# Hidden units of a mixture-of-experts layer dealt to partitions, weight loads in halves, and products of ones at the start

## The chip, the cores and the metric

The kernel runs on one core of a Trainium2 chip. Five engines work side by side there: TensorE (PE, with its weight loads shown apart as PEld), VectorE (DVE), ScalarE (ACT), GpSimd (POOL) and SyncE (SP), which issues most of the DMAs. The metric is the device time of one execution in microseconds (us). Smaller is better.

## The reference

One block of a diffusion-style transformer, all in fp32, on x of 8 sequences of 512 tokens with 256 channels:

```python
mod = (silu(c) @ wmod).reshape(8, 6, 1, 256)      # sa, ca, ga, sb, cb, gb
ga = (2 * (ga >= 0) - 1) * maximum(abs(ga), 0.25)  # gb in the same way
h = layernorm(x) * (1 + ca) + sa
x = x + ga * linear_attention(h)                   # 16 heads of 16, rope, elu + 1, causal
h = layernorm(x) * (1 + cb) + sb
x = x + gb * experts(h)                            # 8 experts, the best 2 of each token
```

An expert is `gelu(h @ w1[e]) @ w2[e]` with w1 of 256 x 1024 and w2 of 1024 x 256. The router's softmax gives each token two experts and their weights, which are normalised to a sum of 1.

## The kernel before

**Attention.** A sequence is worked on in four chunks of 128 tokens. Each chunk goes through `early` (normalise, transpose, project to q, k, v, rope, elu), `middle` (cumulative sums for the denominator, transposes), `late` (scores, state, outputs, the output projection) and `rows_of` (the second normalisation, one row per token for the experts, router logits). After the fourth chunk `route` finds the two experts of each token and scatters its rows by indirect DMA (POOL) into lists by expert in HBM, called `slots`.

**Experts.** A block is one unit of 128 rows (a single) or two (a pair) of one expert's list. `fetch` (L1289) issues on SP the block's weights (`weights1` L1302, `weights2` L1307: 1 MB each) and its rows (L1324). `turn_rows` transposes the rows on DVE. Then, in `experts` (L1448), groups of products make h_ps (inner units on partitions, tokens along the free dimension), ACT applies gelu into g, and `second` (L1369) multiplies g with w2 into y_ps. `finish` scales y and POOL adds it by indirect DMA to the tokens in HBM. The weights have three buffers each. Of the 40 blocks that run, 27 are pairs and 13 are singles; the second half of the execution is experts alone, the first half attention with some experts in between.

**How the inner units lie.** w1 is loaded as [128 channels, 2, 1024]; the stationary operand of a product is 128 neighbouring columns, `w1_sb[:, k, ts(each * j + i, P)]`. So inner unit n*128 + p lies on partition p of the n-th group, and w2 is loaded to match: partition p takes eight rows of 1 KB each, 128 rows apart.

**Startup.** `modulation` (L622) multiplies silu(c) by wmod in two parts. The second part (modr_ps) gives the gates and the second shift and scale: a copy by ACT, then five POOL instructions (add 1 to one quarter; sign, twice; maximum; product), and a store to HBM (modd), from which each sequence loads its rows.

**What sets the order.** Nothing is issued in source order. The class `Plan` (L159) collects all work with a cost in us, a level (smaller goes first) and what it depends on; its `run` (L233) goes through time once, gives each engine the ready work of the smallest level for which buffers are free, and the instructions are issued in that order, engine by engine. A changed cost, level or buffer anywhere can thus move instructions on every engine. PSUM has three groups of banks: `early` (3), `late` (4), `y` (1).

Of the kernel before, what the change touches and what calls it, by code (L numbers as in the profile page):

```python
# [18 lines left out]
P = 128  # L19
HEADS = 16  # L20
# [6 lines left out]
FLOOR = 0.25  # L27
LARGE = 2.0**96
XS = 4

LEVEL = {
    "open": 0, "early": 0, "middle": 0, "late": 0, "rows": 0, "route": 0, "scatter": 0, "plan": 0
# [126 lines left out]
class Plan:  # L159
    SIGNAL = 0.25  # L160
    NEXT = {"DVE": 0.08, "ACT": 0.1}
    DRAIN = {"PE": 0.16}
    TABLE = 1.3
    RATE = 0.26

    def __init__(self, tc, before=None):
        self.tc, self.works, self.level, self.open = tc, [], 0, None
# [65 lines left out]
    def run(self):  # L233
        for w in self.works:
            w.behind -= self.before
            w.waits = len(w.behind)
            for b in w.behind:
                b.ahead.append(w)
            for t in w.tiles:
                t.left = len(t.users)  # L240
        slots = {}
        for w in self.works:
            for t in w.tiles:
                slots.setdefault((id(t.pool), t.tag), t.bufs)
        free = {e: 0.0 for e in {w.engine for w in self.works}}
        ready = {e: [] for e in free}
        events, table, channel, order, clock = [], None, 0.0, [], 0.0

        port = {"DVE": 0.0, "POOL": 0.0}
        for w in self.works:  # L250
            if not w.waits:
                heappush(ready[w.engine], w)
        todo = len(self.works)
        while todo or events:
            for e in sorted(ready):
                if free[e] > clock or not ready[e]:
                    continue
                passed, chosen = [], None
                while ready[e]:
                    w = heappop(ready[e])  # L260
                    if w.port and e == "DVE" and port["POOL"] > clock:
                        passed.append(w)
                        continue
                    need = {}
                    for t in w.tiles:
                        if not t.held:
                            k = (id(t.pool), t.tag)
                            need[k] = need.get(k, 0) + 1
                    if all(slots[k] >= n for k, n in need.items()):
                        chosen = w  # L270
                        break
                    passed.append(w)
                for p_ in passed:
                    heappush(ready[e], p_)
                if chosen is None:
                    continue
                w = chosen
                for t in w.tiles:
                    if not t.held:
                        t.held = True  # L280
                        slots[(id(t.pool), t.tag)] -= 1
                us = w.us
                if w.table is not None and w.table != table:
                    us += self.TABLE
                    table = w.table
                if w.port:
                    if e == "POOL":
                        us += max(port["DVE"] - clock, 0.0)
                    port[e] = clock + us
                free[e] = clock + max(us - self.NEXT.get(e, 0.0), 0.0)  # L290
                w.start, w.stop = clock, clock + us + self.DRAIN.get(e, 0.0)
                if w.bytes:
                    channel = max(channel, w.stop + w.landing) + w.bytes / self.RATE
                    done = channel
                else:
                    done = w.stop + w.landing
                heappush(events, (done, 0, w.at, w))
                heappush(events, (done + self.SIGNAL, 1, w.at, w))
                heappush(events, (free[e], 2, w.at, None))
                order.append(w)  # L300
                todo -= 1
            if not events:
                if todo:
                    left = sorted(w.at for w in self.works if not hasattr(w, "start"))
                    raise RuntimeError(f"no way on: {todo} left, first {left[:5]}")
                break
            clock = events[0][0]
            while events and events[0][0] <= clock:
                _, kind, _, w = heappop(events)
                if kind == 0:  # L310
                    for t in w.tiles:
                        t.left -= 1
                        if not t.left:
                            slots[(id(t.pool), t.tag)] += 1
                    for a in w.ahead:
                        if a.engine == w.engine and not w.bytes:
                            a.waits -= 1
                            if not a.waits:
                                heappush(ready[a.engine], a)
                elif kind == 1:  # L320
                    for a in w.ahead:
                        if a.engine != w.engine or w.bytes:
                            a.waits -= 1
                            if not a.waits:
                                heappush(ready[a.engine], a)
        self.order = order
        return order
# [25 lines left out]
def kernel(  # L353
# [78 lines left out]
    def bank(name, tag, bufs):  # L432
        return L.tile(ps, [P, 512], tag, name, bufs)
# [4 lines left out]
    def early_bank(name):  # L438
        return bank(name, "early", 3)
# [22 lines left out]
    def pool(method, out_, *args, us=None, **kw):  # L462
        if us is None:
            us = 0.12 + 0.0024 * out_.free
        return L.call("POOL", us, method, out_, *args, port=method in two, **kw)

    def copy(out_, in_):
        return L.call("ACT", 0.22 + 0.00075 * out_.free, A.copy, out_, in_)

    def product(out_, a, b, **kw):  # L470
        L.call("PE", 0.0, T.matmul, out_, a, b, **kw)
# [130 lines left out]
    nc.vector.memset(zeros, 0.0)  # L602


    silu = L.tile(cpool, [P, KD, Q], "silu", "silu")
    nc.vector.memset(silu.now(), 0.0)

# [14 lines left out]
    def modulation():  # L622
# [18 lines left out]
        with L.group("PE", 1.1):  # L641
            for k in range(KD):
                for j in range(P // Q):
# [2 lines left out]
                        wm[k][:, (2 + rows_by[j]) * D : (3 + rows_by[j]) * D].of(1),  # L646
                        start=(k == 0), stop=(k == KD - 1), skip_group_check=True,
                    )
        copy(modr, r_ps[:, :D])
        one_more = modr[quarters[rows_by.index(CB)]].of("cb")  # L650
        pool(G.tensor_scalar_add, one_more, one_more, 1.0)

        sgn, mag = (L.tile(p2, [P, D], "sm", t, 4) for t in ("sgn", "mag"))
        sgn, mag, g = sgn[: 2 * Q], mag[: 2 * Q], modr[: 2 * Q].of("g")
        act(mag, g, AF.Abs)
        pool(G.tensor_scalar, sgn, g, 0.0, 2.0, op0=ALU.is_ge, op1=ALU.mult)
        pool(G.tensor_scalar_add, sgn, sgn, -1.0)
        pool(G.tensor_scalar_max, mag, mag, FLOOR)
        pool(G.tensor_mul, g, sgn, mag)
        modded = L.tile(dram, [1, 1], "modded", "modded")  # L660

        def store():
# [12 lines left out]

        stored = L.do("SP", 2.0, store, r=[modr], w=[modded], landing=2.5)
        return modded, stored


    def moments(xs_, n, name):  # L680
# [105 lines left out]
    def middle(q, c):  # L786
# [9 lines left out]
                product(cum_ps[:, :D], ones, q.ksum, start=False, stop=True)  # L796
        q3 = q_.rearrange("p (h d) -> p h d", d=HD)
        dve(V.tensor_mul, qk, cum_ps[:, :D].rearrange("p (h d) -> p h d", d=HD), q3)
        den = L.tile(p2, [P, HEADS, 1], "den", f"den_{n}", 2)
        dve(V.tensor_reduce, den, qk, us=0.42, axis=AX.X, op=ALU.add)  # L800

        dve(V.reciprocal, den, den, us=0.24)
# [26 lines left out]
    def late(q, c):  # L829
# [21 lines left out]

        nxt = None
        if c < NC - 1:
            st_ps = early_bank(f"st_ps_{n}")
            kv = L.tile(p2, [P, KD, PAIR], "kv", f"kv_{n}", 2)
            with L.group("PE", 0.26, hold=[kv]):
                for g in range(KD):
# [43 lines left out]
                        )  # L901
        q.state = nxt
        copy(oT, oT_ps[:, :D])
        a_ps = early_bank(f"a_ps_{n}")
        with L.group("PE", 0.86):
            for k in range(KD):
                product(
# [377 lines left out]

    X = Expert()
    TOP = -50

    def fetch(block):  # L1289
        n, nt = block.n, block.nt  # L1290
# [6 lines left out]
        r = L.tile(pb, [P, 2, ROW - D], "r", f"r_{n}", 3)  # L1297
        reg = {}

        def weights1():  # L1300
            reg["e"] = nc.sync.value_load(block.expert_i.now(), min_val=0, max_val=E - 1)
            nc.sync.dma_start(  # L1302
                out=w1_sb.now(), in_=w1[ds(reg["e"], 1)].rearrange("o (k p) h -> p (o k) h", p=P)
            )

        def weights2():
            nc.sync.dma_start(  # L1307
                out=w2_sb.now(), in_=w2[ds(reg["e"], 1)].rearrange("o (n p) d -> p (o n) d", p=P)
            )

        def rows():
# [14 lines left out]
                apart(got, [s for s in scattered if s not in needed], "those are of later blocks")  # L1326
                gathered.append(got)

        L.do("SP", 0.6, weights1, r=[block.expert_i], w=[w1_sb], landing=2.0, mb=1.0)
        L.do("SP", 0.4, weights2, r=[block.expert_i], w=[w2_sb], landing=2.0, mb=1.0)  # L1330
        L.do("SP", 1.0, rows, r=[block.slot], w=[sx, r], after=block.seen, landing=2.0, mb=0.35 * nt)
        return block, w1_sb, w2_sb, sx, r

    def turn_rows(fetched):
# [113 lines left out]
    def experts(blocks):  # L1448
# [4 lines left out]
        while X.fetched or X.turned:  # L1453
# [11 lines left out]
            for j in range(groups):  # L1465
# [3 lines left out]
                with L.group("PE", 0.2165 * each * KD * nt, hold=[g]):  # L1469
                    for i in range(each):  # L1470
                        for k in range(KD):
                            product(
                                h_ps[:, i * w : (i + 1) * w], w1_sb[:, k, ts(each * j + i, P)],
                                xT[:, k, :w], start=(k == 0), stop=(k == KD - 1),
                            )
                L.level = TOP
# [131 lines left out]
```

## Time and profile before

| | us |
|---|---|
| median of 13 runs | 790.79 (790.02 to 793.68) |
| the profiled execution | 791.07 |
| its span, first to last instruction | 789.4 |
| PE busy / DVE busy / POOL busy / ACT busy | 753.7 / 383.8 / 317.0 / 283.3 |
| mean granted TensorE clock | 0.986 |

The span is what the engines' instructions cover; 1.7 us of the profiled execution lie around it. A fp32 product appears in the trace as two weight loads (PEld) and two matmuls (PE). A weight load can run while the matmul before it still streams. DMA issues stand on SP's queue (SPq) and are not counted as busy.

### The profile page before, as it was taken

To read this page: it belongs to the slowest core of one execution; us is meant where nothing else is said; L and a number is where in the kernel's file an instruction comes from. 1 tells how busy PE (TensorE), PEld (TensorE's weight loads), DVE (VectorE), ACT (ScalarE), POOL (GpSimd) and SP (SyncE) were. 2 spreads that over 40 slices of the span, in tenths; PEclk is the share of its full clock that TensorE was granted. 3 is DMA by queue.
4 is the path that set the end of the run, shared out by engine and by line. 5 is a ranking of instruction groups with operands and counts; after the bars stand their busy time and mean duration, and the time that the engine had idled before them with its cause. 6 is when DMAs were issued, how large, how long until landed. Compare 5 with 4: busy or idle time off the path is not lost.

```text
span 789.4 us, 16224 instructions
## 1 busy us (share of the span) xinstructions
PE 753.7 (95%) x5824; PEld 618.7 (78%) x5824; DVE 383.8 (49%) x1315; ACT 283.3 (36%) x584; POOL 317.0 (40%) x482
## 2 busy tenths in 40 slices
PE   5699979999799999999999999999999999999995
PEld 2477657768587787878888888888989889888884
DVE  3888969898597978878463101111111111111110
ACT  4456445657566665564231111111111111111110
POOL 5835643746445383736238421213212122130332
PEclk9899998999999999999999999999999999999998
DMA  7422370886637556546889987876876978879951
GB/s 243 108 57 75 107 223 19 309 233 200 158 110 206 177 191 194 181 132 202 253 222 279 293 233 205 227 209 195 249 210 210 274 220 256 222 207 316 287 104 22
DMA packets 132195, 154.31 MB, mean 195 GB/s; under 512 B 43640, under 2 KB 115344, under 8 KB 131984
## 3 DMA queue, kind: packets, MB, share of 16 engines
q1 hardware_dynamic: 116704, 125.24, 52.9%
q0 software_dynamic: 15408, 28.00, 14.0%
q8 instruction: 48, 0.79, 0.4%
q14 instruction: 35, 0.29, 0.1%
HBM read 120.19 MB, written 37.20 MB: 199 GB/s over the span
## 4 chain that ended last, share of the span: by engine, by line
PE 79%; POOL 6%; DMA 6%; DVE 4%; issue 3%; SPq 1%; ACT 1%; POOLq 0%; DVEq 0%
PE h_ps L225 26%; PE y_ps L225 25%; PE qk_ps L225 5%; PE oT_ps L225 5%; PE s_ps L225 4%; PE v_ps L225 4%; DMA out_dram<-y,to 3%; PE a_ps L225 3%; PE cum_ps L225 3%; PE qkT_ps L225 2%; DVE sm L225 2%; DMA out_dram<-acc 2%; POOL out_dram L1412 1%; POOL slots L1044 1%; POOL f L225 1%
## 5 line engine op out<-in xcount | busy, mean ns | idle before, releaser
L225 PE MATMUL h_ps<-xT,w 128*128 128x256 f32 (+1 forms) x1280 | 255.1, 346 | 0.0
L225 PE MATMUL y_ps<-w,g 128*128 128x256 f32 x1072 | 253.9, 380 | 0.0
L225 PEld LDWEIGHTS h_ps<-xT,w 128*128 128x128 f32 x1280 | 213.1, 191 | 24.5 <-issue 1.4
L225 PEld LDWEIGHTS y_ps<-w,g 128*128 128x128 f32 x1072 | 201.8, 190 | 27.1 <-issue 0.4
L225 ACT ACTIVATE g<-h_ps 128x512 f32<-128x512 f32 x134 | 80.0, 597 | 327.2 <-PE h_ps L225 327.1
L1412 POOL DMA_INDIRECT acc<-y,to x56 | 89.3, 1595 | 230.9 <-DVE y L225 193.2
L225 DVE SCALAR_TENSOR_TENSOR y<-y_ps,cw,r 128x256 f32<-128x256 f32 x67 | 30.0, 480 | 161.5 <-PE y_ps L225 161.4
L225 DVE STREAM_TRANSPOSE xT<-sx 128x512 f32<-128x512 f32 (+1 forms) x40 | 25.0, 624 | 150.9 <-PE h_ps L225 82.6
L225 DVE TENSOR_TENSOR sm<-s_ps,causal 128x512 f32<-128x512 f32 x128 | 83.1, 681 | 9.7 <-PE s_ps L225 9.6
L1044 POOL DMA_INDIRECT slots<-row,slot x64 | 64.1, 1002 | 27.3 <-issue 13.1
L225 PE MATMUL qk_ps<-wqkv_sb,hT 128*128 128x512 f32 x128 | 62.4, 611 | 0.7 <-DVE qk L225 0.5
L225 POOL TENSOR_TENSOR f<-f,t 128x512 f32<-128x512 f32 x32 | 43.0, 1344 | 37.8 <-DVE t L225 30.3
L225 PEld LDWEIGHTS s_ps<-qT,kT 32*128 32x128 f32 x1024 | 33.3, 194 | 10.4 <-issue 9.9
L225 ACT ACT_TABLE_LOAD x31 | 39.8, 1283 | 4.5 <-DMA cs<-in_cT_dram 3.1
L1412 POOL DMA_INDIRECT out_dram<-y,to x11 | 17.1, 1555 | 56.6 <-DMA out_dram<-acc 22.9
L225 PE MATMUL s_ps<-qT,kT 32*128 32x128 f32 x1024 | 39.6, 292 | 0.0
L225 PE MATMUL oT_ps<-sm,vz 128*32 128x128 f32 x1024 | 37.4, 277 | 1.6 <-DVE sm L225 1.4
L225 PEld LDWEIGHTS qk_ps<-wqkv_sb,hT 128*128 128x128 f32 x128 | 23.4, 194 | 19.3 <-issue 16.0
L225 PE MATMUL v_ps<-wqkv_sb,hT 128*128 128x256 f32 x128 | 36.1, 405 | 1.9 <-ACT hT L225 1.1
L225 PEld LDWEIGHTS oT_ps<-sm,vz 128*32 128x32 f32 x1024 | 27.2, 109 | 11.3 <-issue 7.2
L225 PE MATMUL a_ps<-wo,oT 128*128 128x256 f32 x128 | 33.7, 386 | 0.0
L225 ACT ACTIVATE t<-f 128x512 f32<-128x512 f32 x32 | 20.3, 634 | 33.3 <-POOL f L225 33.3
(229 smaller groups left out, 878.1 us busy)
## 6 DMA issues: line engine op xcount, KB each, us to landing
w<-in_w_dram SPq DMA_DIRECT2D x80, 1024.0 KB, 6.8
r<-slots SPq DMA_DIRECT2D x27, 265.0 KB, 6.3
sx<-slots SPq DMA_DIRECT2D x108, 64.0 KB, 5.2
row<-modd SPq DMA_DIRECT2D x8, 512.0 KB, 9.6
acc<-x SPq DMA_DIRECT2D x8, 512.0 KB, 2.9
out_dram<-acc SPq DMA_DIRECT2D x8, 512.0 KB, 10.5
x<-in_x_dram SPq DMA_DIRECT2D x7, 512.0 KB, 5.3
mod<-modd SPq DMA_DIRECT2D x8, 384.0 KB, 5.0
```

The lines of the kernel that those rows point to most:

```text
L225: return method(now(out), *[now(a) for a in args], **{k: now(a) for k, a in kw.items()})
L1044: s = nc.gpsimd.indirect_dma_start(out=slots, out_offset=IndirectOffsetOnAxis(ap=slot.now()[:, c, j : j + 1], axis=0), in_=row.now()[:, c, ...
L1412: s = nc.gpsimd.indirect_dma_start(out=out.rearrange("b s d -> (b s) d") if block.at_end else acc, out_offset=IndirectOffsetOnAxis(ap=to.n ...
```

## The change

Five things are edited.

1. **Units dealt to partitions.** A stationary operand of h_ps is now every eighth column of w1, `w1_sb[:, k, each * j + i :: NH]` (NH = 8), so that inner unit p*8 + n lies on partition p. Partition p of w2 then takes rows 8p to 8p+7, neighbours in HBM: pieces of 4 KB for a half.
2. **Weights in halves.** Each of w1 and w2 is loaded by two DMAs of 512 KB, at level 900 where it was -50; the planner's costs of the SP work change, it gets a starting time for each engine and holds SP back when over 5 us of DMA are outstanding.
3. **Products of ones.** Ten groups of two products `ones` by `ones` (128x128) on PE, level 0.5, into the bank of y_ps.
4. **Modulation.** The copy of modr_ps takes a bias that adds 1 to the last quarter; the five POOL instructions become three on DVE.
5. **Banks.** The denominator `den` lies in 16 free columns of cum_ps (PSUM) where it was a tile in SBUF; st_ps and a_ps come from the `late` banks where they came from the `early` ones.

```diff
+    BEGIN = {"SP": 0.8}
+    BACKLOG = 5.0
...
-        free = {e: 0.0 for e in {w.engine for w in self.works}}
+        free = {e: self.BEGIN.get(e, 1.7) for e in {w.engine for w in self.works}}
...
+                    if e == "SP":
+                        free[e] = max(free[e], channel - self.BACKLOG)
...
-        copy(modr, r_ps[:, :D])
-        one_more = modr[quarters[rows_by.index(CB)]].of("cb")
-        pool(G.tensor_scalar_add, one_more, one_more, 1.0)
+        act(modr, r_ps[:, :D], AF.Identity, us=0.45, bias=one_more)
...
-        pool(G.tensor_scalar, sgn, g, 0.0, 2.0, op0=ALU.is_ge, op1=ALU.mult)
-        pool(G.tensor_scalar_add, sgn, sgn, -1.0)
-        pool(G.tensor_scalar_max, mag, mag, FLOOR)
-        pool(G.tensor_mul, g, sgn, mag)
+        dve(V.tensor_scalar, sgn, g, 0.0, 2.0, op0=ALU.is_ge, op1=ALU.mult)
+        dve(V.tensor_scalar_max, mag, mag, FLOOR)
+        dve(V.scalar_tensor_tensor, g, sgn, -1.0, mag, op0=ALU.add, op1=ALU.mult)
...
+    L.level = 0.5
+    warm_ps = bank("warm_ps", "y", 1)
+    for i in range(WARM):
+        with L.group("PE", 0.6):
+            for k in range(2):
+                product(warm_ps[:, ts(k, P)], ones, ones, start=True, stop=True)
...
-        den = L.tile(p2, [P, HEADS, 1], "den", f"den_{n}", 2)
+        den = cum_ps[:, D : D + HEADS].unsqueeze(2)
...
-            st_ps = early_bank(f"st_ps_{n}")
+            st_ps = late_bank(f"st_ps_{n}")
...
-        a_ps = early_bank(f"a_ps_{n}")
+        a_ps = late_bank(f"a_ps_{n}")
...
+        def weights1(k):
             nc.sync.dma_start(
-                out=w1_sb.now(), in_=w1[ds(reg["e"], 1)].rearrange("o (k p) h -> p (o k) h", p=P)
+                out=w1_sb.now()[:, k, :],
+                in_=w1[ds(expert(), 1), ts(k, P), :].rearrange("o p h -> p (o h)"),
...
+        def weights2(i):
+            part = slice(i * NH // 2, (i + 1) * NH // 2)
             nc.sync.dma_start(
-                out=w2_sb.now(), in_=w2[ds(reg["e"], 1)].rearrange("o (n p) d -> p (o n) d", p=P)
+                out=w2_sb.now()[:, part, :],
+                in_=w2[ds(expert(), 1)].rearrange("o (p n) d -> p (o n) d", p=P)[:, part, :],
...
-        L.do("SP", 0.6, weights1, r=[block.expert_i], w=[w1_sb], landing=2.0, mb=1.0)
-        L.do("SP", 0.4, weights2, r=[block.expert_i], w=[w2_sb], landing=2.0, mb=1.0)
-        L.do("SP", 1.0, rows, r=[block.slot], w=[sx, r], after=block.seen, landing=2.0, mb=0.35 * nt)
+        L.level = WEIGHTS
+        for us, give, sb in ((0.5, weights1, w1_sb), (0.4, weights2, w2_sb)):
+            for i in range(2):
+                L.do(
+                    "SP", us, lambda give=give, i=i: give(i), r=[block.expert_i], w=[sb.of(i)],
+                    landing=2.0, mb=0.5,
+                )
+        L.level = TOP
+        L.do("SP", 1.8, rows, r=[block.slot], w=[sx, r], after=block.seen, landing=2.0, mb=0.35 * nt)
...
-                                h_ps[:, i * w : (i + 1) * w], w1_sb[:, k, ts(each * j + i, P)],
+                                h_ps[:, i * w : (i + 1) * w], w1_sb[:, k, each * j + i :: NH],
```

The instructions as the planner issues them: PE has twelve products of ones ahead of mod_ps, two behind it and six between the first transposes (tp) and the first v_ps; modr_ps comes ahead of the second qk_ps where it came behind it; SP issues 160 weight loads for the 40 blocks where it issued 80; in the part with experts alone PE's order of h_ps and y_ps groups is the same but for one swap near the end.

More of the change, by code (lines that the diff above doesn't have):

```diff
@@ L29 @@
 XS = 4
+WARM = 10
 LEVEL = {
@@ L252, in run @@
                 heappush(ready[w.engine], w)
+        for e in free:
+            heappush(events, (free[e], 2, -1, None))
         todo = len(self.works)
@@ L602 @@
     nc.vector.memset(zeros, 0.0)
+    one_more = cpool.tile([P, 1], F32, tag="one_more", name="one_more")
+    nc.vector.memset(one_more, 0.0)
+    nc.vector.memset(one_more[3 * Q :, :], 1.0)
     silu = L.tile(cpool, [P, KD, Q], "silu", "silu")
@@ L1287 @@
     TOP = -50
+    WEIGHTS = 900
     def fetch(block):
@@ L1298, in fetch, with expert @@
         reg = {}
-        def weights1():
-            reg["e"] = nc.sync.value_load(block.expert_i.now(), min_val=0, max_val=E - 1)
+        def expert():
+            if not reg:
+                reg["e"] = nc.sync.value_load(block.expert_i.now(), min_val=0, max_val=E - 1)
+            return reg["e"]
+        def weights1(k):
             nc.sync.dma_start(
-                out=w1_sb.now(), in_=w1[ds(reg["e"], 1)].rearrange("o (k p) h -> p (o k) h", p=P)
-            )
-        def weights2():
+                out=w1_sb.now()[:, k, :],
+                in_=w1[ds(expert(), 1), ts(k, P), :].rearrange("o p h -> p (o h)"),
+            )
+        def weights2(i):
+            part = slice(i * NH // 2, (i + 1) * NH // 2)
             nc.sync.dma_start(
-                out=w2_sb.now(), in_=w2[ds(reg["e"], 1)].rearrange("o (n p) d -> p (o n) d", p=P)
+                out=w2_sb.now()[:, part, :],
+                in_=w2[ds(expert(), 1)].rearrange("o (p n) d -> p (o n) d", p=P)[:, part, :],
             )
```

## Prediction

> **What bounds the kernel now.** First the page's head and its two slice rows for TensorE, then the table of busy time by stretches.
>
> ```profile
> span 789.4 us, 16224 instructions
> ...
> PE   5699979999799999999999999999999999999995
> ...
> PEclk9899998999999999999999999999999999999998
> ```
>
> ```profile
> 13.40:30.50 17.10, 12.38 (x70) 6.28 (x68) 13.52 (x44) 9.32 (x19) 12.09 (x14) 1.00 0.29 88
> 30.50:37.30 6.80, 4.32 (x64) 3.57 (x55) 3.70 (x5) 4.47 (x12) 6.64 (x8) 0.50 0.76 145
> 37.30:80.00 42.70, 42.55 (x541) 30.29 (x544) 37.03 (x89) 24.58 (x65) 17.95 (x26) 1.00 0.27 81
> 80.00:240.00 160.00, 147.57 (x1644) 110.82 (x1637) 135.05 (x471) 89.47 (x195) 85.61 (x131) 0.97 0.57 174
> 380.00:780.70 400.70, 400.70 (x1976) 353.41 (x1972) 78.42 (x318) 72.18 (x121) 108.72 (x148) 1.00 0.80 227
> ```
>
> The columns are length, then busy us of PE, PEld, DVE, ACT, POOL, the granted clock, DMA share, GB/s. From 380 to 780.7 PE is busy in every us. So PE bounds, and a change can gain only in four places: PE's idle time (789.4 - 753.7 = 35.7 us, of which 8.7 are the tail behind the last product), half clock, the time of a product, or the tail. Of the idle 27.0, 14.3 lie before 37.3 and 160.00 - 147.57 = 12.4 between 80 and 240. The list of PE's waits names the longest:
>
> ```profile
> PE qkT_ps L225 <- DVE f L225: 6.9, 2, 3.5
> PE mod_ps L225 <- DMA wmod<-in_wmod_dram: 5.2, 2, 5.1
> PE l_ps L225 <- ACT rT L225: 4.0, 1, 4.0
> PE st_ps L225 <- POOL mv_a L225: 2.5, 1, 2.5
> ```
>
> (Total, times, longest.) No row there names expert weights: PE never waits for them. Half clock is seen in the second stretch (0.50), and before 13.4 in durations, though the clock column shows 1.00 there: the same four v_ps matmuls take 2.07 us at 9.11 and 1.13 at 14.86.
>
> **Units dealt to partitions.** This touches what fills most of the time, so it comes first. 1280 loads of h_ps now read every eighth fp32 column, a step of 32 bytes. What hides a load is the matmul before it. The rows, kept apart by form:
>
> ```profile
> L225 PEld LDWEIGHTS h_ps<-xT,w 128*128 128x128 f32 x1280 | 213.1, 191 | 24.5 <-issue 1.4 <-ACT hT L225 0.2 <-ACT t L225 0.2
> L225 PEld LDWEIGHTS oT_ps<-sm,vz 128*32 128x32 f32 x1024 | 27.2, 109 | 11.3 <-issue 7.2 <-DVE sm L225 2.8 <-PE rt_ps L225 0.7
> L225 PEld LDWEIGHTS rt_ps<-ident,row 128*128 128x128 f32 x64 | 8.4, 146 | 6.7 <-issue 3.8 <-ACT t L225 0.5 <-DVE sm L225 0.5
> L225 PE MATMUL h_ps<-xT,w 128*128 128x256 f32 x864 | 203.7, 379 | 0.0
> L225 PE MATMUL h_ps<-xT,w 128*128 128x128 f32 x416 | 51.5, 277 | 0.0
> ```
>
> Of h_ps's matmuls 864 belong to pairs, 416 to singles. In the timeline a pair's eight take 1.73 us, 216 ns each; a single's sixteen go from 557.32 to 559.10, 111 each. A load has a fixed part and a part by columns: 32 columns take 109 ns, 128 take 191, so 82 / 96 = 0.85 ns a column, 109 ns for 128. Today a single's load just fits under its 111, a pair's has 107 to spare.
>
> Does the step slow it? No row shows TensorE reading with such a step. Two rows bound it. Below: the loads of transposes (rt_ps) take 128 fp32 columns in 146, (146 - 109) / 96 = 0.39 ns a column. So the read can run 2.2 times as fast as a product's load uses; a step that halves the read would give 0.78, under today's 0.85. Price 0 (a gain is excluded: the matmuls set the pace). Above: VectorE has one fp32 reduction with exactly this step, plan_begun, beside a contiguous one of the same 40 elements:
>
> ```profile
> L225 DVE TENSOR_REDUCE plan_begun<-is_of x1: 219/219/219, 139.2 to 139.2; 128x8 f32<-128x40 f32 x1
> L225 DVE TENSOR_REDUCE plan_at<-plan_part x1: 190/190/190, 139.4 to 139.4; 128x5 f32<-128x40 f32 x1
> ```
>
> At 8 elements they take 148 and 163. So (219 - 148) / 32 = 2.2 ns an element with the step, (190 - 163) / 32 = 0.8 to 1.0 without: about twice. Twice on the load's 0.85 is 218 ns: singles (218 - 111) x 416 = 44.5 us, pairs (218 - 216) x 864 = 1.7, sum 46. The 2.2 ns itself on TensorE, 282 ns: 71 + 57 = 128. [...]
>
> [...]
>
> The other half of this edit is the DMA. w1 (pieces of 4 KB) lands 5.0 us after its issue in the median, w2 (1 KB) 7.8: w2 gains 2.8 x 40, all hidden, as PE waits for no weights. If that cover were gone, it would be worth as much.
>
> **Weights in halves.** 80 more DMAs of 0.39 us and some 0.07 of register work: 37 us more on SP's queue. SP stands 153.9 us in L1307's and 138.9 in L1302's waits for free buffers, which covers it. Queued behind are the block's rows (sx, r); for xT the DVE waits 82.6 us on PE and 64.4 on rows, but xT is made a block ahead (13.8 us for a pair), and PE has no wait on it. Cost 0; if a block came late, one stall like l_ps's, 4.0.
>
> **Products of ones.** Twenty, each 0.222 us at full clock (1.78 / 8), 0.444 at half. Twelve stand ahead of mod_ps: 2.7 to 5.3 us, from about 1.2 (ones is written by 1.16) to 3.9 or 6.5. PE idles until 5.06 and mod_ps has its second half of wmod only at 5.90, so mod_ps moves 0 to 1.0 later. Six ahead of v_ps, 1.3, beside the 0.8 in which ACT makes hT: 0.5 late. In return full clock comes before v_ps and qk_ps: v_ps 1.87 to 0.96 (starts 9.11, 10.98; 14.86, 15.82), qk_ps 2.95 to 1.81, tp 0.69 to 0.38: 2.4. POOL's first mv_a comes ahead of four small instructions (4.81 to 6.03, 1.1 us), which PE's first transposes wait for. Sum 2.4 + 1.1 - 0.5: **-3**.
>
> **Modulation.** POOL's five instructions take 1.40 + 1.10 + 1.00 + 0.87 + 0.72 = 5.09 us, 20.47 to 25.74. Behind them wait POOL's additions f, then ACT, then DVE, then PE's qkT_ps (3.35 idle to 29.68) and, behind mv_a, st_ps (2.48 to 34.10). The first stall brings half clock on, 4.32 busy us of which half, 2.2, is lost. Together 8.0. DVE takes three instructions of about 0.4 (row<-row,mod, 128x256, takes 0.42): 1.3. What is late next is DVE, busy 13.5 of 17.1. I take **-5**, between 0 and -8. modd is stored about 5 us sooner (25.76 before), and so the gate rows of the first sequence.
>
> **Banks.** den in PSUM: one more DVE operand from there, 0.48 against 0.42 (y<-y_ps, scaled) x 32 = 2 us on DVE, hidden behind PE; it also holds the cum_ps bank about 1.5 us longer. st_ps (24) and a_ps (32) now wait for a bank that s_ps frees: PE's waits on DVE sm are 1.9 us in all. Cost 0, at most 2.
>
> **The new order.** Between 80 and 240 it is another one. Recoverable there: 12.4 idle, and half clock at 119 to 126 and 211 to 215 (0.97 x 160: 4.8 lost). Which stalls return can't be read from the order; a new one can be as large as l_ps's 4.0 with its half clock. I take **-3**, between -10 and +6. The tail (8.7) stays: its chain of additions is untouched.
>
> **Sum.** Against the profiled 791.07 (span 789.4 and 1.7 around; the median 790.79 is 0.3 less): 791.07 - 3 - 5 - 3 = **780**. Bounds of the three: -3 + 1 and -1; 0 to -8; +6 to -10: 768 to 790 or so.
>
> **Rivals.**
> - *The step slows the weight loads* (slower). Place: singles' h_ps, 416 loads that have 111 ns. It decides from 111 + 11 / 416 us = 137 ns a load, 1.07 ns a column. At twice today's rate +46: 826 (814 to 836). For it: VectorE's two rows. Against: the transposes' loads. With VectorE's own 2.2 ns, +128: 908, and the part with experts alone slows too.
> - *The stalls come back elsewhere* (same): the startup's gain is eaten because DVE, 135 of 160 us busy between 80 and 240, is no sooner done. 790.
> - *Warm products do not warm*: full clock comes as late as before; then -1 instead of -3: 782, within the forecast's own range.
>
> **Numbers.** A measurement of this kernel tells about 0.2% from no change, 1.6 us. Free loads with fewer stalls, 768 to 789: 0.56. Same: 0.05. Loads at twice, 792 to 838: 0.27; still slower: 0.08; free loads but more stalls, 793 to 800: 0.04. Faster 0.56, same 0.05, slower 0.39. The forecast's own range is 768 to 789; with the rival it is 769 to 838, leaving out about 0.12.
>
> **What would show it.** Right: h_ps's load row stays at 191, a single's sixteen matmuls at 1.78; v_ps's first four take about 1.1; no PE wait of over 3 us before 37; w2's landing near 5. Wrong: the load row near 300, with h_ps of singles at 3.5 us a group and VectorE's rows proven the better guide; or new PE waits on sm, rT or rows between 80 and 240 of more than 12 us.

## The result, and the profile after

The changed kernel takes 863.67 us in the median of 10 runs (860.25 to 867.04), the kernel before 791.81 on the same chips (46 runs): a ratio of 1.0906, 95% interval 1.089 to 1.0922. The forecast was 780, within 769 to 838. It is wrong in sign, and the range did not hold the time. The profiled execution took 866.23 us. First the head of its page (busy time, then slices):

```profile
span 864.5 us, 16569 instructions
...
PE 834.9 (97%) x5864; PEld 721.1 (83%) x5864; DVE 388.7 (45%) x1320; ACT 281.7 (33%) x582; POOL 312.1 (36%) x478
...
PE   8898979989999999999999999999999999999996
...
PEclk9999989999999999999999999999999999999999
```

TensorE (PE) is now busy for 834.9 us where it was 753.7, and idle for 864.5 - 834.9 = 29.6 where it was 35.7. So the idle time did fall, by 6.0 before rounding; the time was lost while PE was busy. Some of the groups that the prediction showed, kept apart by form, with those of the products of ones:

```profile
L228 PEld LDWEIGHTS h_ps<-xT,w 128*128 128x128 f32 x1280 | 316.5, 334 | 4.7 <-ACT hT L228 0.8 <-PE tp L228 0.5 <-issue 0.2
L228 PE MATMUL h_ps<-xT,w 128*128 128x256 f32 x864 | 224.8, 403 | 0.0
L228 PE MATMUL h_ps<-xT,w 128*128 128x128 f32 x416 | 102.8, 401 | 0.9 <-ACT hT L228 0.7 <-PE tp L228 0.3
L228 PE MATMUL warm_ps<-ones 128*128 128x128 f32 x40 | 7.4, 359 | 1.2 <-DVE ones L540 1.2
```

A weight load of h_ps takes 334 ns where it took 191. The matmuls of singles, which had just covered it, go from 51.5 to 102.8 us, those of pairs from 203.7 to 224.8: 72.5 by the sum of the two forms (255.1 to 327.6). The products of ones add 7.4, all other matmuls together 1.3. So 72.5 + 8.7 - 6.0 = 75.2, which is the whole of 866.23 - 791.07. The timeline says how a pair's group became longer; the columns are start, length and what ran:

```profile
629.93 2.08 PE L228 MATMUL h_ps<-xT,w 128*128 128x256 f32 x8
631.84 1.89 PE L228 MATMUL y_ps<-w,g 128*128 128x256 f32 x8
633.57 2.08 PE L228 MATMUL h_ps<-xT,w 128*128 128x256 f32 x8
```

From start to start, eight products of h_ps take 631.84 - 629.93 = 1.91 us, 240 ns each, and eight of y_ps, whose loads are contiguous, 633.57 - 631.84 = 1.73 us, 216 each. A load with the step thus needs 240 ns in a stream: 1.87 ns for each of its 128 columns, 2.2 times the 0.85 that the prediction estimated for a contiguous one. A pair's matmul has 216 to cover it, a single's 111.

The stretches that the prediction used, and the longest of PE's waits (total, times, longest):

```profile
13.40:30.50 17.10, 14.16 (x99) 7.37 (x97) 13.67 (x41) 9.21 (x20) 9.46 (x11) 0.90 0.48 132
...
80.00:240.00 160.00, 147.63 (x1492) 110.69 (x1493) 124.56 (x415) 78.18 (x178) 75.00 (x116) 0.95 0.50 154
380.00:780.70 400.70, 400.70 (x2007) 375.97 (x2006) 93.81 (x383) 71.96 (x126) 110.80 (x156) 1.00 0.72 212
```

```profile
PE v_ps L228 <- ACT kT L228: 5.1, 2, 4.1
PE oT_ps L228 <- DVE sm L228: 4.0, 12, 1.1
PE qkT_ps L228 <- DVE f L228: 2.4, 1, 2.4
PE v_ps L228 <- DVE t L228: 2.3, 1, 2.3
```

In the first stretch PE is busy for 14.16 of 17.10 us (12.38 before), and the waits behind the modulation's POOL work are gone or halved. Up to 37.3 PE's idle time falls from 14.3 to 5.0 us; 4.1 of that come back between 37.3 and 80 (0.2 to 4.2, no wait above 1.1) and 1.0 between 240 and 380. Between 80 and 240 the idle time is the same 12.4 as before, on other operands (the v_ps wait of 4.1 lies at 116), and the clock is 0.95 (0.97 before). From 380 to 780.7 PE is never idle in either kernel: there every us that h_ps's matmuls become longer moves the end.

### The profile page after: what moved, and what is told of

Its sections match the earlier page's. It is cut to its first block, busy times and chain, and to the rows that moved or that the text cites. A ratio compares the mean times of both kernels' runs of the same rounds, so it can differ in the third digit from the quotient of the medians.

```text
span 864.5 us, 16569 instructions
## 1 busy us (share of the span) xinstructions
PE 834.9 (97%) x5864; PEld 721.1 (83%) x5864; DVE 388.7 (45%) x1320; ACT 281.7 (33%) x582; POOL 312.1 (36%) x478
## 5 line engine op out<-in xcount | busy, mean ns | idle before, releaser
L228 PE MATMUL h_ps<-xT,w 128*128 128x256 f32 (+1 forms) x1280 | 327.6, 403 | 0.9 <-ACT hT L228 0.7
L228 PEld LDWEIGHTS h_ps<-xT,w 128*128 128x128 f32 x1280 | 316.5, 334 | 4.7 <-ACT hT L228 0.8
L228 PE MATMUL qk_ps<-wqkv_sb,hT 128*128 128x512 f32 x128 | 65.3, 634 | 1.1 <-ACT hT L228 0.7
L228 PE MATMUL v_ps<-wqkv_sb,hT 128*128 128x256 f32 x128 | 35.7, 402 | 7.7 <-ACT kT L228 5.1
L228 PE MATMUL oT_ps<-sm,vz 128*32 128x128 f32 x1024 | 39.8, 285 | 2.1 <-DVE sm L228 2.0
L228 ACT ACT_TABLE_LOAD x29 | 37.2, 1283 | 4.8 <-DMA cs<-in_cT_dram 3.1
L228 PEld LDWEIGHTS v_ps<-wqkv_sb,hT 128*128 128x128 f32 x128 | 22.6, 194 | 12.4 <-ACT kT L228 5.5
```

The costliest lines, as they stand in the source:

```text
L228: return method(now(out), *[now(a) for a in args], **{k: now(a) for k, a in kw.items()})
```

## Experiments

**The theory** after the result: reading a stationary operand with a step of 32 bytes slows the weight load (334 ns against 191), and nothing else matters much. **The rivals**: the other layout of w2, the halves or the new order cost the time; or the loss is the step's, but only from some larger step on.

**Undoing the step, and doing it alone.** On the chip that ran these two and the next two, the kernel before took 855.31 us, not 792, so each run is compared with the kernel before on its own chip.

```diff
 rest_contiguous: the changed kernel with
-  in_=w2[ds(expert(), 1)].rearrange("o (p n) d -> p (o n) d", p=P)[:, part, :],
+  in_=w2[ds(expert(), 1)].rearrange("o (n p) d -> p (o n) d", p=P)[:, part, :],
-  h_ps[:, i * w : (i + 1) * w], w1_sb[:, k, each * j + i :: NH],
+  h_ps[:, i * w : (i + 1) * w], w1_sb[:, k, ts(each * j + i, P)],
 only_step: the kernel before with the same two edits the other way round (w2 there is one DMA, in pieces of 8 KB)
```

> The whole change without its first part: a stationary operand is again 128 neighbouring columns of w1, and w2 lies to match (pieces of 1 KB); halves, products of ones, modulation and banks stay. Theory (the step of 32 bytes alone slows the weight loads, 334 ns against 191, and all of h_ps's growth from 255 to 328 us is its): the h_ps load returns to 191 ns, h_ps to 255 us, and the time to 866 - 72.5 = 794, with the stalls of the new order open: 785 to 797. Rival (the loads are slowed by the weights' DMAs in halves or in 4 KB pieces, which write SBUF beside them): loads stay above 250 ns and the time above 830.

Measured: 860.68, ratio 1.0074 (1.0045 to 1.0102). The loads are back at 192 ns. The times expected were those of a chip with 792 us, so here the ratio and the loads count.

> The kernel before with the first part alone: every eighth column of w1 as the stationary operand, w2 in pieces of 8 KB, each still one DMA of 1 MB. Theory (the step): h_ps's load 334 ns, a pair's matmul at 240 ns where it was 216, a single's at 247 where it was 111; 864 x 24 + 416 x 136 ns = 77 us, less what stalls between 80 and 240 are filled: 855 to 870. Rival (halves and order): load 191, time 785 to 795.

Measured: 908.03, ratio 1.0625 (1.0588 to 1.0663). Its rows are those of the changed kernel:

```profile
L225 PEld LDWEIGHTS h_ps<-xT,w 128*128 128x128 f32 x1280 | 316.4, 334 | 11.6 <-issue 7.8 <-ACT kT L225 0.8
L225 PE MATMUL h_ps<-xT,w 128*128 128x256 f32 x864 | 224.3, 403 | 0.0
L225 PE MATMUL h_ps<-xT,w 128*128 128x128 f32 x416 | 104.1, 403 | 6.2 <-issue 5.8 <-ACT kT L225 0.4
```

The dealt units, with whole weights and the planner as before, make the loss; the rivals of the halves and of the new order fall. w2's layout changed here too, so the rival of its pieces is left to the probe below. The loss is 52.7 us here, less than the 73 by which the rows of h_ps grow; more on that below.

**Other steps.** The units are dealt in groups of 2 or 4, so that a stationary operand has a step of 8 or 16 bytes, and w2's rows are loaded to match:

```diff
 step_of_2 (STEP = 2), step_of_4 (STEP = 4): the changed kernel with
+    def columns(n):
+        first = n // STEP * STEP * P + n % STEP
+        return slice(first, first + (P - 1) * STEP + 1, STEP)
-  out=w2_sb.now()[:, part, :],
-  in_=w2[ds(expert(), 1)].rearrange("o (p n) d -> p (o n) d", p=P)[:, part, :],
+  out=w2_sb.now()[:, part, :].rearrange("p (m s) d -> p m (s d)", s=STEP),
+  in_=w2[ds(expert(), 1)].rearrange("o (m p s) d -> p (o m) (s d)", p=P, s=STEP)[
+      :, i * NH // 2 // STEP : (i + 1) * NH // 2 // STEP, :],
-  w1_sb[:, k, each * j + i :: NH],
+  w1_sb[:, k, columns(each * j + i)],
```

> The whole change, but units dealt by fours: the stationary operand is every fourth column (16 bytes), w2 still in pieces of 4 KB for a half. [...] If the price grows with the step: a load of 240 to 300 ns and 815 to 850. If 16 bytes are still free: 191 ns and the time of the run with neighbouring columns.

Measured: 911.74, ratio 1.0669 (1.0625 to 1.0713); a load takes 328 ns, above the 240 to 300 of a price that grows with the step and near the 334 at 32 bytes.

> The whole change, but units dealt by twos: every second column (8 bytes), w2 in pieces of 2 KB. [...] If each step costs: load between 191 and 334, and 800 to 850.

Measured: 861.32, ratio 1.0082 (1.0059 to 1.0105); a load takes 197 ns:

```profile
L229 PEld LDWEIGHTS h_ps<-xT,w 128*128 128x128 f32 x1280 | 222.3, 197 | 20.2 <-ACT hT L229 0.8 <-PE tp L229 0.5 <-issue 0.2
L229 PE MATMUL h_ps<-xT,w 128*128 128x256 f32 x864 | 204.5, 380 | 0.0
L229 PE MATMUL h_ps<-xT,w 128*128 128x128 f32 x416 | 54.1, 284 | 1.0 <-ACT hT L229 0.7 <-PE tp L229 0.3
```

So a step of 8 bytes is nearly free (197 ns against 192), and one of 16 costs nearly all that 32 does (328 against 334): the loads grow by 131 ns between 8 and 16 bytes and by 6 between 16 and 32.

**The disputed cost by itself.** In the kernel with contiguous units, the products of ones give way to groups of eight products or transposes that read a wide tile of ones with a given step (the edit is shortened):

```diff
 probe: rest_contiguous with
-    warm_ps ... ten groups of two products of ones
+    wide = L.tile(wpool, [P, 16 * P], "w2", "wide", 3)
+    dve(V.memset, wide, 1.0)
...
+    product(out_[:, ts(i % 4, P)], wide[:, : (P - 1) * step + 1 : step], ones)       # load a to h
+    product(out_[:, ts(i % 2, 2 * P)], ones, wide[:, : (2 * P - 1) * step + 1 : step])  # move a to d
+    turn(out_[:, ts(i % 4, P)], wide[:, : (P - 1) * step + 1 : step])                # turn a to c
```

> The kernel with the contiguous units, in which the products of ones are replaced by groups of eight products (stationary operand from a tile of ones, every 1st, 2nd, 3rd, 4th, 5th, 6th, 8th or 16th fp32 column; 128 columns moving), by groups of eight with 256 moving columns of step 1, 2, 4, 8, and by groups of eight transposes with step 1, 4, 8. Nothing is left out. [...] Rival (only a product's weight load is slow by the step, for example in its two passes): the moving operands' and transposes' rows stay as they are at step 1. Rival (it grows with the distance): 16 well above 8, 8 well above 4.

Measured, in the groups by form (loada to loadh are steps 1, 2, 3, 4, 5, 6, 8, 16; movea to moved 1, 2, 4, 8; turna to turnc 1, 4, 8):

```profile
L228 PEld LDWEIGHTS loada_ps<-ones,wide 128*128 128x128 f32 x16 | 1.9, 191 | 0.2 <-issue 0.2
L228 PEld LDWEIGHTS loadb_ps<-ones,wide 128*128 128x128 f32 x16 | 2.0, 196 | 0.1
L228 PEld LDWEIGHTS loadc_ps<-ones,wide 128*128 128x128 f32 x16 | 2.9, 260 | 0.0
L228 PEld LDWEIGHTS loadd_ps<-ones,wide 128*128 128x128 f32 x16 | 3.9, 327 | 0.4 <-issue 0.2
L228 PEld LDWEIGHTS loadg_ps<-ones,wide 128*128 128x128 f32 x16 | 3.9, 334 | 0.1
L228 PEld LDWEIGHTS loadh_ps<-ones,wide 128*128 128x128 f32 x16 | 3.6, 309 | 0.0
L228 PE MATMUL movea_ps<-wide,ones 128*128 128x256 f32 x16 | 3.6, 379 | 0.0
L228 PE MATMUL moveb_ps<-wide,ones 128*128 128x256 f32 x16 | 3.8, 388 | 0.0
L228 PE MATMUL movec_ps<-wide,ones 128*128 128x256 f32 x16 | 7.5, 634 | 0.0
L228 PEld LDWEIGHTS turna_ps<-ident,wide 128*128 128x128 f32 x8 | 0.9, 140 | 0.2 <-issue 0.2
L228 PEld LDWEIGHTS turnc_ps<-ident,wide 128*128 128x128 f32 x8 | 1.0, 187 | 0.5 <-issue 0.5
```

The load's mean is 191 and 196 ns at 4 and 8 bytes, 260 at 12, 327 at 16, 334 at 32 and 309 at 64: from 16 bytes on these no longer grow with the distance. A moving operand does the same: sixteen matmuls take 3.6 us at 4 bytes, 3.8 at 8 and 7.5 at 16. The transposes' loads become longer too, 140 ns at 4 bytes to 187 at 32. So the step slows all three kinds of read that were measured, the first two mostly between 8 and 16 bytes (196 to 327 ns, 388 to 634), and neither rival holds. Nor is it the transfers beside the loads: in the stretch of loadd no DMA moves anything (the last two columns), and its loads take 327 ns all the same.

```profile
24.18:27.95 3.77, 3.77 (x21) 3.65 (x23) 3.57 (x13) 0.00 (x0) 1.72 (x3) 1.00 0.00 0
```

With that the rival of w2's layout falls too: here only the step differs from group to group. (The kernel with all these groups takes 842.99 us, one run.)

**The rest of the change.** On the chip of the probe, the kernel before took 793.33 us. There rest_contiguous was measured again, as rest_again; no_ones is the same kernel without the loop of products; ones_alone is the kernel before with that loop.

> The changed kernel with contiguous units again, for the other half of the change (halves, ones, modulation, banks, new order). The prediction's terms: -3 -5 -3, so 0.986 of the kernel before. Rival from the profile of the changed kernel (the rest of its busy time 8.7 up, idle time 6.0 down): +2.7, 1.003 to 1.01 as in the first measurement.

Measured: 791.45, ratio 0.9976 (0.9966 to 0.9986). Against the changed kernel's 1.0906, from other chips with 792 us, that is 0.093, or 74 us, for the dealt units on top of the rest. The same kernel's 1.0074 came from the chip with 855 us.

> The kernel with contiguous units, without the products of ones. The prediction's term (they save 3 us, by full clock before the first projections): 3 us longer than the kernel with contiguous units, the first four v_ps at about 2.07 us again. Rival (they take about as much of TensorE's time as the clock gives back): within 1.5 us of it, PE's busy time about 7 lower and idle time about 7 more.

Measured: 796.41, ratio 1.004 (1.0023 to 1.0056).

> The kernel before with the products of ones alone. The prediction's term: 3 us shorter, 0.996. Rival: 1.000 to 1.003; the clock is full from about 6 us but stalls and half clock further on (behind the modulation's POOL work, which is as before) keep the end where it was.

Measured: 790.25, ratio 0.9962 (0.995 to 0.9974): 3.0 us shorter, as priced. In PE's timeline of ones_alone, the first four v_ps take 0.87 us from start to start where they took 1.87, and the first qkT_ps starts at 27.43 us where it started at 29.68. Without the ones the other edits are 3 us slower than nothing, so their -8 of the prediction did not come.

**Which of the others?** step_again repeats only_step; the other three add one edit, or two, to the kernel before, as the change's diff has them: ones and modulation; den in cum_ps with st_ps and a_ps in the late banks; halves, level 900 and the planner's constants (units contiguous). The chip had the kernel before at 852.04.

> The kernel before with the dealt units alone, again. Theory (the step doubles the weight load, and where TensorE is never idle the end moves by its whole row): h_ps's matmul rows 224 and 104 us, sum 73 more than in the kernel before, and the end 70 to 75 later, about 1.09. Rival (about 20 of the 73 lie beside waits, as 1.0625 in the first measurement suggests): 1.06 to 1.07.

> The kernel before with the products of ones and the new modulation, without the rest. The prediction's terms: -3 and -5, 0.990 of the kernel before, PE's 3.35 and 2.48 waits behind the modulation's POOL work gone or halved. Rival (the waits go to other operands, DVE being the next that is late): the same as with the ones alone, 0.996.

> The kernel before with den in cum_ps and st_ps and a_ps in the late banks. The prediction's term: 0 to +2 us, 1.000 to 1.0025. Rival (st_ps and a_ps wait for banks that s_ps and oT_ps hold, which the waits on DVE sm rising from 1.9 to 4.0 us in the changed kernel suggest): +2 to +5, 1.003 to 1.006, with more PE waits on sm.

> The kernel before with weights in halves at level 900 and the planner's new constants, units contiguous. The prediction's terms: 0 for the halves, -3 (-10 to +6) for the new order. Rival (the new order moves stalls and makes them no shorter): +1 to +5, 1.001 to 1.006.

Measured: step_again 1.0622 (1.0583 to 1.066), ones_and_modulation 0.985 (0.9822 to 0.9878), banks_alone 0.9865 (0.9839 to 0.9892), halves_alone 0.9994 (0.9963 to 1.0024). The first fits its rival: on such a chip the step costs 54 us although the matmul rows of h_ps rise as elsewhere (to 224.3 and 105.4). The next two gain more than any theory had for them; what else is different on this chip stands in the last section. Since the chip differs, the three were measured again, with one more: the kernel before with ones, modulation and banks, but without halves and new constants. The chip had the kernel before at 792.80.

> The kernel before with the products of ones and the new modulation, without the rest; on a chip on which the kernel before takes about 792 us. The prediction's terms -3 and -5: 0.990. Rival (the waits go to other operands): 0.996 as with the ones alone. On a chip on which it takes about 852 the ratio 0.985 should come again.

> The kernel before with den in cum_ps and st_ps and a_ps in the late banks. The prediction's term: 1.000 to 1.0025. Rival from the first measurement: 0.9865 whichever chip it is. Third: slower by 2 to 5 us on a chip with the kernel before at 792.

> The kernel before with weights in halves at level 900 and the planner's new constants, units contiguous. The prediction's terms: 0 - 3: 0.996. Since the kernel with everything but the dealt units came to 0.9976, this one has to carry what the ones (-3) and the modulation gain and that kernel does not show: +3 to +8, 1.004 to 1.010. Rival (the banks carry it): 1.000.

> The kernel before with ones, modulation and banks, weights whole at their old level and the planner's old constants, units contiguous. If the halves and the new constants carry the loss: the sum of the parts, -6 to -10, 0.987 to 0.992. If the banks carry it: 0.9976 or more, as for the kernel with the halves too.

| kernel before with | ratio (95%) | us against before |
|---|---|---|
| ones (the probe's chip) | 0.9962 (0.995 to 0.9974) | -3.0 |
| ones, modulation | 1.0035 (1.0019 to 1.005) | +2.8 |
| banks | 1.0053 (1.0034 to 1.0072) | +4.2 |
| halves, level, constants | 1.008 (1.0054 to 1.0107) | +6.3 |
| ones, modulation, banks | 0.9892 (0.9871 to 0.9912) | -8.6 |
| all of these (the probe's chip) | 0.9976 (0.9966 to 0.9986) | -1.9 |

The last column is the ratio less one, by 792.8 us (793.3 on the probe's chip). The parts do not add: +2.8 and +4.2 together give -8.6. Where the time goes shows in the stretches of ones_alone, modulation_2 and startup_and_banks (length, then busy us of PE, PEld, DVE, ACT, POOL, clock, DMA share, GB/s):

```profile
0.00:40.00 40.00, 29.85 (x226) 21.19 (x228) 24.82 (x79) 18.19 (x40) 28.80 (x62) 0.87 0.70 183
40.00:80.00 40.00, 39.79 (x506) 27.92 (x497) 34.56 (x82) 23.93 (x64) 17.73 (x25) 1.00 0.21 56
80.00:240.00 160.00, 147.92 (x1657) 110.59 (x1660) 140.51 (x475) 89.55 (x195) 87.09 (x136) 0.99 0.59 181
240.00:380.00 140.00, 139.92 (x1544) 112.02 (x1545) 110.78 (x367) 79.58 (x166) 73.26 (x112) 1.00 0.62 183
```

```profile
0.00:40.00 40.00, 34.54 (x271) 24.81 (x272) 27.89 (x86) 19.47 (x43) 24.72 (x57) 0.91 0.69 196
40.00:80.00 40.00, 38.65 (x468) 26.24 (x470) 34.25 (x86) 21.77 (x57) 16.01 (x24) 1.00 0.13 43
80.00:240.00 160.00, 145.86 (x1631) 109.70 (x1620) 131.32 (x457) 82.85 (x189) 85.78 (x137) 0.99 0.60 182
240.00:380.00 140.00, 139.39 (x1488) 110.06 (x1487) 110.71 (x367) 80.91 (x166) 71.81 (x109) 1.00 0.59 185
```

```profile
0.00:40.00 40.00, 34.21 (x280) 23.75 (x280) 30.09 (x91) 21.46 (x48) 24.95 (x58) 1.00 0.73 199
...
80.00:240.00 160.00, 151.63 (x1663) 115.37 (x1663) 136.65 (x477) 91.47 (x205) 91.86 (x143) 0.98 0.62 190
240.00:380.00 140.00, 136.17 (x1407) 108.32 (x1406) 104.53 (x351) 73.14 (x151) 66.46 (x103) 0.98 0.60 180
```

With the new modulation, PE's idle time in the first 40 us falls from 10.15 to 5.46: the 4.7 that the prediction wanted. Between 80 and 240 it rises from 12.1 to 14.1, between 40 and 80 by 1.1 and between 240 and 380 by 0.5, and PE's busy time is 4.3 larger over the whole (759.7 against 755.4), of which 2.6 in oT_ps (37.2 to 39.8). With the banks as well, 80 to 240 has 8.4 idle and 240 to 380 has 3.8. Each set of edits is another order of attention and experts; what in the order makes the difference is not shown.

startup_and_banks is 1.1% faster than the kernel before on this chip: 784.44 us against 792.80. It is the version to keep of those measured, though only on one chip.

## Why the prediction was wrong

**Units dealt to partitions: the step that failed is "Price 0".** Of the prices 0, 46 and 128 the forecast has the first, with the transposes' loads as proof of a reserve ("so the read can run 2.2 times as fast as a product's load uses"). That the two kinds of load have the same limit no row showed, and the probe shows no reserve. The step slows each kind of load from the rate it had: a product's from at most 111 ns in a stream to 240 (334 where its row was 191), a transpose's row from 140 ns to 187 (at 32 bytes). The transposes' row told how fast another kind of load goes, not how much a product's load has to spare; and its 0.39 ns a column took the fixed part from products' loads, as no row shows a transpose's load of 32 columns. The point from which the rival was to decide (137 ns a load) is passed by far: 240.

**The rival's size.** Its place, the singles, was right, but "twice" gave 46 us. Measured were 72.5: 51.3 in the singles (44.5 priced) and 21.1 in the pairs (1.7 priced), because the load came to 240 ns in a stream, not 218. A pair's matmul covers 216 of it: at 218 nearly all, at 240 it leaves 24 ns open, 864 times. The rows of VectorE, 2.2 against 0.8 to 1.0 ns, had a factor of 2.2 to 2.75 in them; rounding it to two cost 26 of the 72. A high end of 838 was taken from the rounded value, while the 908 of the other bound was left outside.

**The DMA half** was right in being hidden. The halves of w2 land 5.2 us after their issue and those of w1 4.5 (7.8 and 5.0 before, for transfers twice as large), and neither kernel shows a wait of PE on weights. The 72.5 us that the loads cost were spent on a transfer for which PE never waited.

**Products of ones, -3:** right, -3.0 alone (0.9962), and with the rest about -5 (0.9976 against 1.004).

**Modulation, -5:** right at its place (4.7 us of idle time gone before 40), wrong at the end: 1.0035 with the ones against 0.9962 without it, 5.8 us the other way, across two chips. The rival "the stalls come back elsewhere" holds for 3.7 us of idle time that return between 40 and 380; the rest is PE's busy time, 4.3 us longer, which neither the prediction nor the rival had, and no run shows why it grew.

**Banks, 0 to +2:** +4.2 alone, but -11.3 on top of ones and modulation (0.9892 against 1.0035). No single price fits both.

**Weights in halves 0, new order -3:** +6.3 alone, and some +6.7 beside the others (0.9976 against 0.9892, two chips). Nothing shows the halves themselves to cost: PE waits for no weights. That the order does it is argued, not shown; it wasn't tried with halves in the old order.

**The sum of the rest** was -11 and came to -1.9. The bounds of the three terms, as they stand, add up to -22 to +4, so to 769 to 795 and not to "768 to 790 or so"; -1.9 lies inside. Likewise the 0.12 for times outside 769 to 838 counts 0.04 for 793 to 800, which lie inside. The tail behind PE's last product, which was to stay at 8.7 us, is 9.0 in rest_again and 7.0 in the changed kernel.

Open stays what decides between a gain and a loss for one order, and why the kernel before takes 792 us on some chips and 852 to 855 on others.

## What to carry to other kernels

Before a stationary or moving operand is read with a step, set its step beside those measured here: in a stream, a load of 128 fp32 columns with its matmul took 118 ns at a step of 4 bytes, 124 at 8, 169 at 12 and 211 to 244 from 16 to 64 (240 in the changed kernel, at 32), and the row of a matmul that moves 256 columns 379, 388 and 634 ns at 4, 8 and 16. Compare the load with the matmul that covers it, form by form (here 216 ns of a pair's, 111 of a single's). A gain in DMA pieces is worth nothing where the engine that bounds the kernel does not wait for that transfer: here w2 landed after 5.2 us instead of 7.8, and PE had no wait on weights in either kernel. Where a planner sets the order, a small edit's own saving is smaller than the shift it gives to the order (one edit's worth here went from -11 to +4 with its company), so each set of edits has to be measured together, on more than one chip.

## What the runs showed of the hardware that was not expected

- In the probe's timeline, from the start of a group to the start of what follows, an fp32 load of 128 columns with its matmul takes 118 and 124 ns at steps of 4 and 8 bytes, 169 at 12, 231 at 16, 244 at 32 and 211 at 64: from 16 bytes on distance adds at most 13 ns. Moving operands become longer in the same place (379, 388, 634 and 643 ns of a matmul with 256 columns for steps of 4, 8, 16 and 32 bytes).
- A transpose's load with a step of 32 bytes is longer (187 against 140 ns), but eight transposes still take 0.97 us from start to start of what follows, against 0.93: the longer load is covered there.
- The same kernel took 792 to 793 us on some chips and 852 to 855 on two others, where its mean granted clock was 0.96 and not 0.98, and edits that cost 0.4 to 0.5% on the former gained 1.4 to 1.5% on the latter. In all eight traces from those two chips, ScalarE and VectorE pause at times with a releaser that the profile calls remote and can't name, ScalarE for 25 to 67 us in all; so in halves_alone:

```profile
ACT g L228 <- remote: 19.6, 4, 6.6
...
ACT oT L228 <- remote: 15.0, 2, 8.5
...
ACT qT L228 <- remote: 11.0, 2, 10.6
```

The ten traces from the other chips have no such row. So the kernels on those two chips were held up by something that the profile doesn't name, and the step's 53 to 54 us there, like the gains of 1.4 to 1.5%, may owe something to it. That is argued, not shown: the kernel before has no trace from such a chip, and what lies behind the pauses is not settled.
